# Self attention's rounded rows: turned as float32 with the rounding constant in them, and the maxima scaled by ScalarE

## The chip, the cores and the metric

The kernel runs on one core of one Trainium2 chip. The metric is the device time of one execution in microseconds (us), as the median of several runs. The engines are named as in the profile: PE is TensorE (PEld is its weight load), DVE is VectorE, ACT is ScalarE, POOL is GpSimd, SP is SyncE, which only issues transfers.

## The reference, cut to what matters

The model is a decoder of two layers on 16 sequences of 128 tokens and 512 features: a state space layer, a cross attention and a feed-forward layer, then a self attention, a gated cross attention and a mixture of experts; after each the input is added and a layer norm taken. The change lies in the self attention alone. It has 16 query heads and 4 key and value heads of 32 features, and its four projections are "bitlinear": weights of -1, 0 and 1 times a scale, and activations rounded to 8 bits by row.

```python
def bitlinear(x, W):
    sw = jnp.mean(jnp.abs(W)) + 1e-05
    Wq = jnp.clip(jnp.round(W / sw), -1.0, 1.0) * sw
    sx = 127.0 / jnp.clip(jnp.max(jnp.abs(x), axis=-1, keepdims=True), 1e-05, None)
    xq = jnp.clip(jnp.round(x * sx), -128.0, 127.0) / sx
    return jnp.einsum('bsd,od->bso', xq, Wq)
...
scores = jnp.einsum('bkgsd,bktd->bkgst', qg, k) * scale
scores = jnp.where(causal[None, None, None], jnp.asarray(-jnp.inf, scores.dtype), scores)
p = jax.nn.softmax(scores, axis=-1)
out = jnp.einsum('bkgst,bktd->bkgsd', p, v)
...
return bitlinear(out, Wo)
```

## The kernel before, in words

The 16 sequences stay in SBUF as tiles of 128 tokens by 512 features (k.x), and the layers run as stages one after the other: the state space layer, the cross attention, the feed-forward layer (stage_ffn), the two attentions of the second layer together (stage_attention) and the experts.

stage_attention works on 16 pairs of sequences: eight pairs of the class SelfAttention (L1158), then eight of GatedAttention (L1376). Each pair has eight units (two sequences by four groups of heads), and one loop (L1553) walks over all units. In one turn of the loop, unit t has its exponentials taken (exps, on ACT), the unit before has its probabilities turned on PE and copied out of PSUM (turn), the maxima are taken for units t+1 and t+2 where t+1 is even (top, two units at once, on DVE), and the scores are multiplied for units t+2 and t+3 where t+2 is even (scores, on PE). Beside that, jobs written as generators move on by one step in each turn: project() for a pair that begins 14 units ahead of its own units, values() for each half of a pair that is done, and output() at its end. A yield is the end of a step. Tiles come from rings of buffers: a tag with 2 buffers lets the third tile of that tag in only when the readers of the first are done. The order of the instructions on each engine is fixed at compile time by a planner, which starts from the order in which they are written and fills gaps that it expects; where an instruction must not move, the code says so (keep_in_program_order).

The pieces that the change touches:

- levels (L1188) rounds the rows of two sequences to 8 bits. It is called twice for a pair: by project() on the inputs, and by output() on the attention's result, so 16 times. DVE takes the largest magnitude of each row (L1194), works out the scale (L1195 to L1198), and writes x times the scale plus MAGIC, 12582912.0, into the float32 tile q_t (L1203): in float32 this sum has no fraction left, which is the rounding. ACT adds minus MAGIC and writes bfloat16 (tile q_q, L1207). PE turns the eight blocks of 128 by 128 as bfloat16 into one PSUM tile, ptq (L1212), and ACT copies that tile of 128x1024 to SBUF as q_T (L1215). The projections (L1233, L1256, L1368) use q_T as weights.
- The PSUM tag pp has two buffers of one bank. In stage_attention all of these live in it, one after the other: ptq, pkv (L1230), two pq (L1254), ptk (L1270), two pt (L1260), and two po (L1366). The other six banks hold two score tiles of two banks each (sc0 and sc2), the turned probabilities (pt, in a pool of their own) and the attention's product (ao).
- top (L1300) takes the maximum of two units' scores on DVE (L1303) and multiplies it by nal, the negative scale of the row, on DVE (L1304). exps (L1307) uses the result as the bias of its exponentials (L1313). GatedAttention does the same multiplication on ACT (L1476).
- turn (L1322) copies a unit's turned probabilities out of PSUM. Units whose number is a multiple of DVE_TURNS go to DVE (L1330), the others to ACT (L1328). With DVE_TURNS = 4 that is units 0 and 4 of each pair.
- The levels and the projections of pairs 0 and 1 are put into the last part of stage_ffn (attention(), L986). There the tiles have other homes: q_q lies in the ring xn of that stage.

transpose4 (L565) is a helper that turns four blocks of 128x128 with the float32 identity; its instructions all carry L568.

Of the kernel before, what the change touches and what calls it, by code (L numbers as in the profile page):

```python
# [10 lines left out]
F32 = mybir.dt.float32  # L11
BF16 = mybir.dt.bfloat16
# [3 lines left out]
AF = mybir.ActivationFunctionType  # L16
ALU = mybir.AluOpType
# [3 lines left out]
P = 128  # L21
NB = 16
D = 512
KC = D // P
# [540 lines left out]
def transpose4(k, psum_tile, src):  # L565

    for c in range(4):
        k.nc.tensor.transpose(psum_tile[:, c * P : (c + 1) * P], src[:, c * P : (c + 1) * P], k.ident)  # L568
# [56 lines left out]
def stage_xattn(k):  # L625
# [9 lines left out]
    with ExitStack() as ctx:  # L635
# [224 lines left out]
        for t in range(-12, len(units) + 4):  # L860
            for lag, what in ((3, turn), (2, norm), (1, exps), (0, top), (-1, scores)):
                if not 0 <= t - lag < len(units):
                    continue
                b, g, i = units[t - lag]
                st = state[b]
                if what is scores and (g, i) == (0, 0):
                    st.b, st.sc, st.mx, st.pr, st.sm, st.pTs = b, {}, {}, {}, {}, {}
                what(st, g, i)
                if what is turn and i == 1:
                    running.append(outputs(st, g))  # L870
            if t == len(units) - 6:
                running.append(ffn_weights())
            if t == len(units) - 4:
                running.append(prepare_first())
            b, r = divmod(t + 11, U)
            if r == 0 and b < NB:
                running.append(project(b))
            if (t + 13) % (2 * U) == 0 and t > 0 and (t + 13) // (2 * U) < NB // 2:
                running.append(norm_inputs((t + 13) // (2 * U)))
            b, r = divmod(t + 15, U)  # L880
            if r == 0 and b > 0 and b < NB and b % 4 == 0:
                running.append(angles(b // 4))
            advance()
# [80 lines left out]
def stage_ffn(k):  # L964


    nc, tc = k.nc, k.tc
    LAG = 2
    with ExitStack() as ctx:
        wk = ctx.enter_context(tc.tile_pool(name="s3w", bufs=3))  # L970
# [15 lines left out]
        def attention():  # L986

            bit = k.bit_pool
            homes = [
                dict(q_t=(wk, "q_t", 3), q_q=(wk, "xn", 3), al=(bit, "al", 2), nal=(bit, "nal", 2)) for _ in range(2)  # L990
            ]
            homes[0].update(
                q_T=(wk, "xn", 3), kr1=(wk, "q_q", 3), kr2=(wk, "q_T", 3), qr1=(wk, "xn", 3), qr2=(wk, "q_t", 3),
                sv=(bit, "sv", 1), skT=(bit, "skT", 1), sqT=(bit, "sqT", 2),
            )
            homes[1].update(q_T=(k.early, "q_T", 1))
            k.bit_first = [SelfAttention(k, p, (None, Homes(**h), Homes(pp=(po_, "pp", 2)), None, None, None)) for p, h in enumerate(homes)]
            yield from k.bit_first[0].project()
            k.bit_second = k.bit_first[1].project()
            for _ in range(5):  # L1000
                next(k.bit_second)
                yield

        states = []
        for b0 in range(0, NB, 2):
            st = Ctx() if b0 else k.ffn_first
            st.xs = k.x[b0 : b0 + 2]
            states.append(st)
        late, soon = iter(()), attention()

        def hidden(sn, j):
# [38 lines left out]
        for t in range(len(steps) + LAG):  # L1050
            if t < len(steps):
                n, j = steps[t]
# [5 lines left out]
            if t >= LAG:  # L1058
                m, i = steps[t - LAG]
# [98 lines left out]
class SelfAttention:  # L1158
# [4 lines left out]
    HD = 32  # L1163
    SCALE = 1.0 / math.sqrt(HD)
    LAG = 1
    DVE_TURNS = 4

    def __init__(self, k, p, pools):
        self.k, self.nc, self.xs = k, k.nc, k.x[2 * p : 2 * p + 2]
# [18 lines left out]
    def levels(self, ins, out):  # L1188

        nc, small = self.nc, self.k.small  # L1190
        s = small.tile([P, 2], F32, tag="qs2", name="qs")
        out.step = small.tile([P, 2], F32, tag="qst2", name="qst")
        for i, x in enumerate(ins):
            nc.vector.tensor_reduce(s[:, i : i + 1], x, AX.X, ALU.max, apply_absolute_value=True)  # L1194
        nc.vector.tensor_scalar(s, s, 1e-5, None, ALU.max)  # L1195
        nc.vector.reciprocal(s, s)
        nc.vector.tensor_scalar(s, s, 127.0, None, ALU.mult)
        nc.vector.reciprocal(out.step, s)  # L1198
        yield
        ts = []  # L1200
        for i, x in enumerate(ins):
            ts.append(self.wr.tile([P, D], F32, tag="q_t", name="q_t"))
            nc.vector.tensor_scalar(ts[i], x, s[:, i : i + 1], MAGIC, ALU.mult, ALU.add)  # L1203
        yield
        q = self.wr.tile([P, 2, D], BF16, tag="q_q", name="q_q")
        for i in range(2):
            nc.scalar.activation(q[:, i], ts[i], AF.Identity, bias=self.k.nmagic)  # L1207
        yield
        pt = self.pp.tile([P, 2 * KC, P], BF16, tag="pp", name="ptq")
        for i in range(2):  # L1210
            for c in range(KC):
                nc.tensor.transpose(pt[:, KC * i + c], q[:, i, c * P : (c + 1) * P], self.k.identb)  # L1212
        yield
        out.qT = self.wr.tile([P, 2 * KC, P], BF16, tag="q_T", name="q_T")
        nc.scalar.copy(out.qT, pt)  # L1215

    def project(self):

# [81 lines left out]
    def top(self, n):  # L1300
        nc = self.nc
        mx = self.k.small.tile([P, 2, 4], F32, tag="mx", name="mx")
        nc.vector.tensor_reduce(mx, self.sc2[n], AX.X, ALU.max)  # L1303
        nc.vector.tensor_scalar(mx, mx, self.nal[:, n // 4 : n // 4 + 1], None, ALU.mult)  # L1304
        self.mx[n], self.mx[n + 1] = mx[:, 0], mx[:, 1]

    def exps(self, n):  # L1307
# [14 lines left out]
    def turn(self, n):  # L1322
# [3 lines left out]
        sT = self.sT[n] = self.wk.tile([P, D], F32, tag="at_T", name="at_T", bufs=7)  # L1326
        if n % self.DVE_TURNS:
            nc.scalar.copy(sT, pt)  # L1328
# [47 lines left out]
class GatedAttention:  # L1376
# [7 lines left out]
    LAG = 2  # L1384
    DVE_TURNS = 2

# [210 lines left out]
class Moe:  # L1597
# [95 lines left out]
    def route(self, p):  # L1693
# [27 lines left out]
        for i in range(2):  # L1721
            top = wr.tile([P, 8], F32, tag="r_top", name="r_top", bufs=2)
            nc.vector.max(top, s[:, i])
            nc.vector.match_replace(rest[:, i], top, s[:, i], 0.0)
# [724 lines left out]
```

## Time and profile before

| what | value |
|---|---|
| median of 5 runs | 3019.68 us |
| the five runs | 3001.12, 3001.50, 3019.68, 3021.91, 3023.83 us |
| the profiled execution's own time | 3020.38 us |
| its span | 3018.5 us |
| granted TensorE clock, mean | 0.986 |
| PE busy | 2887.3 us (96%) |
| DVE busy | 1864.2 us (62%) |
| ACT busy | 1335.6 us (44%) |
| POOL busy | 1563.5 us (52%) |

The profile is of one execution, and its time stands 0.7 us above the median. Times inside it are counted from the span's start. The self attention's first scores start at 1659 us and its last exponentials at 1852 us, so nearly all that the change touches lies in 200 us of 3018. The shares of the whole span say little about it; the views by stretch do.

How to read the rows: "x32" is the number of instructions, "mean ns" the duration of one. Instructions of one engine are pipelined, so that one can start before the one ahead of it has ended: what an instruction takes from its engine is the distance from its start to the next one's start, and this is less than its duration. "Idle before" is time in which the engine stood still, with the instruction that ended it.

### The profile page before, as it was taken

How to read it: one execution, taken by the hardware profiler on the slowest of the kernel's cores; microseconds unless marked ns; L12 is line 12 of the kernel's file. 1: busy time of each engine (PE TensorE's matmuls, PEld its weight loads, DVE VectorE, ACT ScalarE, POOL GpSimd, SP SyncE). 2: the span in 40 equal slices, each digit the busy share in tenths (PEclk: the TensorE clock that was granted, in tenths of full speed). 3: DMA queues.
4: the chain of work that ended last, by engine and by line, in shares of the span. 5: the costliest groups of instructions: out<-in, count | busy, mean ns of one | idle time of the engine just before them, and what ended most of it. 6: DMA issues, size and time to landing. Idle time of an engine off the chain costs nothing.

```text
span 3018.5 us, 41723 instructions
## 1 busy us (share of the span) xinstructions
PE 2887.3 (96%) x14446; PEld 1937.2 (64%) x14446; DVE 1864.2 (62%) x4168; ACT 1335.6 (44%) x3297; POOL 1563.5 (52%) x1352
## 2 busy tenths in 40 slices
PE   8999999999999999999999899999999799999988
PEld 6666665555555555555787556666677577777766
DVE  6999997776676686665886897566542312322213
ACT  6887884343343343345444897655422111111112
POOL 7999995434344343332333663266455652343554
PEclk9999999999999999999999999999999999999999
DMA  6755454870000000023000200244366565554653
GB/s 198 216 135 131 134 127 124 282 264 11 7 11 11 7 15 8 11 79 128 1 1 2 69 1 10 66 152 155 132 223 220 204 216 183 188 193 161 206 174 120
DMA packets 177392, 345.23 MB, mean 114 GB/s; under 512 B 25277, under 2 KB 84157, under 8 KB 175638
## 3 DMA queue, kind: packets, MB, share of 16 engines
q1 hardware_dynamic: 126342, 217.64, 23.6%
q0 software_dynamic: 26016, 80.80, 7.9%
q10 hardware_dynamic: 24816, 44.05, 3.9%
q8 instruction: 116, 1.90, 0.3%
q14 instruction: 102, 0.84, 0.1%
HBM read 256.22 MB, written 151.99 MB: 135 GB/s over the span
## 4 chain that ended last, share of the span: by engine, by line
PE 64%; DVE 11%; ACT 3%; issue 2%; another core or an unknown queue 2%; DMA 1%; POOL 1%; SPq 0%; ACTq 0%; DVEq 0%; POOLq 0%
PE y L2069 7%; PE pq L708 7%; PE po L828 6%; PE pu L2033 5%; PE pg L2033 4%; PE po L1040 4%; PE pr L2018 3%; PE ao L817 3%; PE sc L777 3%; PE pt L568 2%; PE pg L1020 2%; PE pu L1020 2%; PE pw L1513 2%; PE ps L1430 2%
## 5 line engine op out<-in xcount | busy, mean ns | idle before, releaser
L797 POOL TENSOR_TENSOR pr<-pr,sm 128x512 f32<-128x512 f32 x128 | 135.3, 1057 | 365.9 <-DVE sm L796 276.9
L66 POOL TENSOR_TENSOR dBx<-dtx,BC 128x1024 f32<-128x1024 f32 (+1 forms) x131 | 300.5, 2315 | 16.6 <-DVE h L66 10.5
L790 ACT ACTIVATE pr<-sc,mx,sf 128x256 f32<-128x256 f32 x256 | 142.2, 560 | 335.5 <-DVE mx L783 296.6
L2092 POOL DMA_INDIRECT got<-results,gidx x126 | 121.0, 961 | 289.0 <-DMA results<-yo 241.6
L66 ACT ACTIVATE h<-dt,negA 128x254 f32<-128x254 f32 x512 | 244.1, 477 | 16.8 <-ACT h L66 0.2
L828 PE MATMUL po<-w,aT 128*128 128x512 f32 x512 | 233.1, 593 | 1.0 <-DVE aT L822 1.0
L708 PE MATMUL pq<-w,xT 128*128 128x512 f32 x512 | 232.0, 596 | 0.0
L2069 PE MATMUL y<-dn,act 128*128 128x512 f32 x372 | 183.2, 616 | 22.6 <-DVE act L2053 13.8
L2104 POOL TENSOR_TENSOR x<-got,x 128x512 f32<-128x512 f32 x134 | 168.4, 1273 | 68.1 <-DMA got<-results,gidx 64.9
L2053 DVE TENSOR_TENSOR act<-pu,act 128x512 f32<-128x512 f32 (+1 forms) x53 | 33.1, 625 | 259.0 <-PE pu L2033 149.7
L679 POOL TENSOR_TENSOR m<-m,m 128x512 f32<-128x512 f32 x96 | 122.5, 1276 | 116.9 <-DVE m L674 113.6
L66 DVE TENSOR_TENSOR_SCAN h<-h,dBx 128x1024 f32<-128x1024 f32 x72 | 164.9, 2290 | 28.0 <-ACT h L66 23.0
L2033 PE MATMUL pu<-xgT,gu 128*128 128x256 f32 (+1 forms) x848 | 174.0, 359 | 0.0
L2033 PE MATMUL pg<-xgT,gu 128*128 128x256 f32 (+1 forms) x848 | 170.4, 354 | 0.0
L66 PE MATMUL pkv<-w,cT 128*128 128x512 f32 x368 | 167.5, 598 | 0.8 <-DMA w<-in_x_wvT 0.5
L1030 POOL TENSOR_TENSOR lo<-sg,hi 128x512 fp32r<-128x512 f32 x64 | 84.2, 1317 | 155.0 <-ACT hi L1029 155.0
L708 PEld LDWEIGHTS pq<-w,xT 128*128 128x128 f32 x512 | 94.7, 191 | 101.5 <-issue 93.8
L2086 DVE TENSOR_SCALAR yo<-y,row 128x512 f32<-128x512 f32 x87 | 65.2, 750 | 152.5 <-PE y L2069 146.3
L828 PEld LDWEIGHTS po<-w,aT 128*128 128x128 f32 x512 | 94.6, 190 | 100.9 <-issue 97.3
L1832 POOL DMA_INDIRECT bucket<-r_row,r_to x126 | 125.2, 994 | 59.4 <-issue 46.9
L2033 PEld LDWEIGHTS pu<-xgT,gu 128*128 128x128 f32 x848 | 145.6, 195 | 15.1
L2033 PEld LDWEIGHTS pg<-xgT,gu 128*128 128x128 f32 x848 | 145.9, 191 | 14.6
(462 smaller groups left out, 6955.8 us busy)
## 6 DMA issues: line engine op xcount, KB each, us to landing
bucket<-zeros SPq DMA_DIRECT2D x88, 388.0 KB
BC<-bcd SPq DMA_DIRECT2D x128, 256.0 KB
row<-bucket SPq DMA_DIRECT2D x39, 776.0 KB
gu<-in_moe_guT SPq DMA_DIRECT2D x16, 1408.0 KB
results<-yo ACTq DMA_DIRECT2D x87, 256.0 KB
x_k<-kv ACTq DMA_DIRECT2D x32, 256.0 KB
x_v<-kv ACTq DMA_DIRECT2D x32, 256.0 KB
v<-x_v SPq DMA_DIRECT2D x32, 256.0 KB
```

The source lines that it names most:

```text
L66: return self.tc.keep_in_program_order(call(*args, **kw))
L679: nc.gpsimd.tensor_tensor(m1, m1, m2, ALU.add)
L708: nc.tensor.matmul(ps, src[:, c], w[c], start=c == 0, stop=c == KC - 1)
L790: nc.scalar.activation(pr[:, j], st.sc[g, i][:, j], AF.Exp, scale=st.sf[:, h : h + 1], bias=st.mx[g, i][:, j : j + 1], accum_out=sm[:, j : ...
L797: nc.gpsimd.tensor_tensor(pr, pr, sm.unsqueeze(2).to_broadcast([P, 2, 2 * P]), ALU.mult)
L828: nc.tensor.matmul(st.po, aT[:, j], k.wo[h // 8][:, h % 8], start=h == 0, stop=h == G * J - 1)
L1020: nc.tensor.matmul(p[:, e], w[:, c, at : at + P], sn.qT[:, :, c], start=c == 0, stop=c == KC - 1)
L1832: return self.nc.gpsimd.indirect_dma_start(out=table[:, :], out_offset=bass.IndirectOffsetOnAxis(ap=to[:, i, g : g + 1], axis=0), in_=row[ ...
L2033: self.nc.tensor.matmul(ps[:, e, 0:n], gu[:, c, at : at + P], u.xT[:, c, 0:n], start=c == 0, stop=c == KC - 1)
L2069: self.k.tc.keep_in_program_order(self.nc.tensor.matmul(y, aT, dn[:, c], start=c == 2, stop=c == 1))
L2092: self.nc.gpsimd.indirect_dma_start(out=got[:, :], out_offset=None, in_=table, in_offset=bass.IndirectOffsetOnAxis(ap=at, axis=0),)
L2104: self.nc.gpsimd.tensor_tensor(self.k.x[b], got, self.k.x[b], ALU.add)
```

## The change

levels no longer makes q_q. PE turns the float32 rows q_t, MAGIC still in them, four blocks to a PSUM tile of 128x512 float32; ACT reads each of the two tiles out of PSUM, adds minus MAGIC and writes the bfloat16 q_T. The number of steps stays: before, a step each for ACT's rounding, for the turning, and then the copy; now a step for the first turning, then the first copy with the second turning, then the second copy. Two pp tiles are taken in place of one. The multiplication of the maxima moves from DVE to ACT. DVE_TURNS goes from 4 to 8, so that only unit 0 of a self attention pair is copied by DVE. GatedAttention has its own DVE_TURNS (2) and its own top, and both stay.

```diff
@@ attention() in stage_ffn
-                dict(q_t=(wk, "q_t", 3), q_q=(wk, "xn", 3), al=(bit, "al", 2), nal=(bit, "nal", 2)) for _ in range(2)
+                dict(q_t=(wk, "q_t", 3), al=(bit, "al", 2), nal=(bit, "nal", 2)) for _ in range(2)
@@ class SelfAttention
-    DVE_TURNS = 4
+    DVE_TURNS = 8
@@ levels
-        q = self.wr.tile([P, 2, D], BF16, tag="q_q", name="q_q")
+        out.qT = self.wr.tile([P, 2 * KC, P], BF16, tag="q_T", name="q_T")
         for i in range(2):
-            nc.scalar.activation(q[:, i], ts[i], AF.Identity, bias=self.k.nmagic)
-        yield
-        pt = self.pp.tile([P, 2 * KC, P], BF16, tag="pp", name="ptq")
-        for i in range(2):
-            for c in range(KC):
-                nc.tensor.transpose(pt[:, KC * i + c], q[:, i, c * P : (c + 1) * P], self.k.identb)
-        yield
-        out.qT = self.wr.tile([P, 2 * KC, P], BF16, tag="q_T", name="q_T")
-        nc.scalar.copy(out.qT, pt)
+            pt = self.pp.tile([P, D], F32, tag="pp", name="ptq")
+            transpose4(self.k, pt, ts[i])
+            yield
+            nc.scalar.activation(
+                out.qT[:, KC * i : KC * i + KC], pt.rearrange("p (c t) -> p c t", c=KC), AF.Identity, bias=self.k.nmagic
+            )
@@ top
-        nc.vector.tensor_scalar(mx, mx, self.nal[:, n // 4 : n // 4 + 1], None, ALU.mult)
+        nc.scalar.mul(mx, mx, self.nal[:, n // 4 : n // 4 + 1])
```

## The prediction

> **What bounds the kernel now.** I read the page's busy shares and chain first.
>
> ```profile
> PE 2887.3 (96%) x14446; PEld 1937.2 (64%) x14446; DVE 1864.2 (62%) x4168; ACT 1335.6 (44%) x3297; POOL 1563.5 (52%) x1352
> ...
> PE 64%; DVE 11%; ACT 3%; issue 2%; another core or an unknown queue 2%; DMA 1%; POOL 1%; SPq 0%; ACTq 0%; DVEq 0%; POOLq 0%
> ```
>
> Over the whole span PE carries the end. The 11% of DVE must lie somewhere, so the next view is busy time by stretch: the end of the feed-forward stage, the middle of the self attention, four pairs' worth of it, and its end.
>
> ```profile
> 1590.00:1660.00 70.00, 68.78 (x464) 54.71 (x463) 45.93 (x111) 28.32 (x48) 26.11 (x22) 1.00 0.01 2
> 1700.00:1817.00 117.00, 105.92 (x892) 68.24 (x893) 113.98 (x311) 111.90 (x273) 82.56 (x116) 1.00 0.01 1
> 1724.00:1817.00 93.00, 84.41 (x708) 54.30 (x705) 92.12 (x261) 89.01 (x218) 63.16 (x90) 1.00 0.01 1
> 1817.00:1852.60 35.60, 34.77 (x236) 22.34 (x229) 26.92 (x97) 26.78 (x67) 12.03 (x20) 1.00 0.01 2
> ```
>
> After the length the columns are PE, PEld, DVE, ACT and POOL. In the first and last row PE is full (1.2 and 0.8 us idle). In the 117 us between, DVE is: 0.9 us idle in 93, where ACT has 4.0 and PE 8.6. The chain of waits over 1700 to 1835 agrees: its shares by line begin with the maxima (L1303) at 15.1%, and seven of the next eight names are DVE's. In order of time it reads like this (start, length, what):
>
> ```profile
> 1763.90 0.66 DVE qr L1182 x2
> 1764.56 1.13 DVE mx L1303
> 1765.69 0.66 DVE x L1370
> ```
>
> So **DVE sets the pace from 1700 to 1817**, one pair in 93/4 = 23.3 us, five pairs' worth; before and after it PE does.
>
> **The change, part by part.** The groups that it touches, by line and shape, in 1724 to 1817 (busy us and mean ns of one behind the bar):
>
> ```profile
> L1207 ACT ACTIVATE q_q<-q_t,nmagic 128x512 bf16<-128x512 f32 x14 | 10.2, 795 | 0.0
> ...
> L1215 ACT COPY q_T<-ptq 128x1024 bf16<-128x1024 bf16 x8 | 8.7, 1090 | 0.0
> ...
> L1304 DVE TENSOR_SCALAR mx<-mx,nal 128x8 f32<-128x8 f32 x16 | 5.5, 341 | 0.0
> ...
> L568 PE MATMUL pt<-ident,qr 128*128 128x128 f32 x32 | 5.0, 279 | 0.0
> ...
> L1212 PE MATMUL ptq<-identb,q_q 128*128 128x128 bf16 x56 | 4.3, 220 | 0.0
> ```
>
> Instructions overlap their neighbours, so I price each by its share of its engine: start to next start in the timeline, averaged over these 93 us. In DVE's timeline:
>
> ```profile
> 1761.83 0.67 DVE L1180 TENSOR_TENSOR qr<-pq,l_cos 128x512 f32<-128x512 f32 x1
> 1762.43 0.21 DVE L1304 TENSOR_SCALAR mx<-mx,nal 128x8 f32<-128x8 f32 x1
> 1762.56 0.74 DVE L1182 TENSOR_TENSOR qr<-pq,l_sin 128x256 f32<-128x256 f32 x2
> ```
>
> The scaling took 0.13 us of DVE here, and another one at 1766.28 took 0.33; their average is 0.257. That of the copy L1330 is 0.598.
>
> *DVE, for four pairs:* 16 scalings leave (16 x 0.257 = 4.1 us) and four of the eight copies (4 x 0.598 = 2.4). Sum -6.5.
>
> *ACT, for four pairs:* eight copies of 128x1024 leave, 0.965 of the engine each: -7.7. The 16 constant-removals stay but read PSUM. None of that shape is here; below stands the plain 128x512 copy out of PSUM (L1344, 0.47), above q_q itself (0.62). The gate's activation L1453, also 128x512 out of PSUM with a pointer operand, took 1882.83 to 1883.40, and I take its 0.57: -0.8. Four copies come from DVE at 0.49: +2.0. The gated attention has the scaling on ACT already (L1476, median 301 ns of 32); in ACT's timeline there:
>
> ```profile
> 1855.95 0.30 ACT L1476 ACTIVATE mx<-mx,r 128x8 f32<-128x8 f32 x1 [2.14 <-DVE mx L1475]
> 1856.34 0.46 ACT L1484 ACTIVATE at_s<-sc,mx,r 128x128 f32<-128x128 f32 x1
> ```
>
> The exponential that reads the result starts 0.39 us after it. Where other work comes between, I bound it below by 0.25 (the 128x128 scalings L1237); I take 0.325, so +5.2 (4.0 to 6.4). Sum -1.3, with ends -4.2 and +0.7. ACT goes from 89.0 to 87.7 of the 93.
>
> *PE, for four pairs:* 64 bfloat16 turnings at 0.067 become float32 ones. The float32 turnings pt took 0.115 and those of the probabilities, some waits in them, 0.144, so +3.1 to +4.9 us; I take 3.1, since pt is the row without probabilities to wait for. PE goes from 84.4 to 87.5.
>
> *Waits.* ACT's scaling must wait for the reduction, as the exponentials do now for L1304 (8.3 us in 11 waits from 1661 to 1853). Behind a scaling that waits stand copies out of PSUM, and PE's turnings and DVE wait for those. In the gated rows ACT stood idle 44.1 us before 21 of 32 scalings, but there it is half empty. Here it ends at 94%, so bounds are 0 and 32 reductions of 1.13 us, 36 us. I take 0: the scaling comes one DVE instruction earlier than now (L1304 stood behind a 0.60 us L1180 above), and this pays for the hop. q_t is now held until PE has turned it, a step longer; its two buffers are refilled three steps later at the earliest, so this costs nothing; if that cover went, the one wait now at L1203 was 0.5 us. The shorter chain from q_t to q_T (one hop less) gains nothing either: project() begins 14 units ahead. The new pp tile is the second rival below. The change issues no transfer and moves past none.
>
> *One rule against it.* The row says that a scaling takes 0.257 of DVE and 0.325 of ACT. The Trainium skill, "ScalarE: Activation LUTs", section "Rules for kernel authors", says to put multiplications on VectorE and not on ScalarE, since VectorE is the faster at them. On the engine's time alone trace and rule agree in sign (+0.07 us each, 1.1 for four pairs). By the rule the edit would be a loss of that much, by the trace it is a gain, because DVE is the engine that is full.
>
> **The sum.** DVE alone would allow 6.5 less in 93 us. But PE at 87.5, with the 2 us in 93 that it idles even where it bounds (1.2 in 70, 0.8 in 36), cannot go below 89.5. So **PE is late next**: 93 - 89.5 = 3.5 us for four pairs, and 3.5 x 117/93 = 4.4 us from 1700 to 1817. Against this, the levels that lie where PE is full already: the inputs of pairs 0 and 1 (1590 to 1660) and about two outputs after 1817. Four levels of eight turnings at 0.048 more: +1.5 us. Net -2.9: 3020.4 - 2.9 = **3017.5** for the profiled execution. That one stood 0.7 above the median; I leave it at 3017.5. The bounds of the price rows move it little: PE's upper end (+4.9) leaves a gain of 2.2 in the middle and a loss of 2.5 at the edges, so no change; DVE's whole 6.5 is a gain of 8.2 - 1.5 = 6.7. Own range 3012 to 3023.
>
> **The rivals.**
>
> *The freed DVE is used whole* (10%). If PE's 87.5 is too high, because its turnings hide behind matmuls of small rows, DVE's 6.5 counts in full, and the part of the stage from 1661 to 1700 gains its share too (DVE 30.6 of 38.6 us occupied there, so little): 3020.4 - 6.7 - 1 = 3012.7. Against it: the busy row above leaves PE 8.6 us, and 5 of them would have to vanish.
>
> *The pp ring takes the place of DVE* (14%, slower). Ten pp tiles a pair become twelve, in two buffers, with PE's queue in order. By the steps of the jobs, two tiles are taken in the same turn in five of eight turns (before, in three), so the first queries (L1256) come to wait for the reader of the tile before. Such waits stand in the list already:
>
> ```profile
> PE pq L1256 <- DVE kr L1244: 2.2, 3, 1.0
> ...
> PE po L1368 <- ACT skT L1275: 1.3, 2, 0.9
> ```
>
> They are 0.65 to 1.0 us each (sum, count, longest). If each of the 32 float32 tiles (16 levels by two) costs 1.0 us of PE, PE in 1661.4 to 1852.6 needs 175.4 + 6.1 (128 x 0.048) + 32 = 213.5 of 191.2 us: +22, so 3042. It decides from 0.3 us a tile, where PE is just full (191.2 - 181.5 = 9.7, over 32), and is slower by more than 0.5% from 0.77. Against it: a tile's reader is written ahead of the next tile's turning.
>
> *Nothing is left* (12%). ACT's upper end, or some of its 36 us of waits, eats DVE's gain: ACT at 89.7 with its present 4.0 idle is again 93.7. Time 3020.4 + 0.7 x 117/93 + 1.5 = 3022.8, up to 3030 if six scalings wait for a whole reduction.
>
> *The other group of runs* (18%). The five runs are two at 3001 and three at 3020 to 3024, and one trace cannot say why. If the median falls among the lower, it is 3001.5 - 2.9 = 2998.6.
>
> **How the numbers follow.** The forecast has 46%. 0.5%, about what a measurement of this kernel can tell from no change, is 15 us. Faster by more than that is only the lower group, 18%; slower only the ring, 14%; the rest, 68%, is within. The range reaches from the lower group with a few us below it (2996) to the end of "nothing is left" (3030), and leaves the ring out.
>
> **What would show it.** Right: between 1700 and 1817 DVE falls from 98% to about 95%, PE rises to 97%, the distance between maxima of neighbouring pairs falls from 23.3 to about 22.4 us; turnings of q_t take 0.115 of PE; ptq to q_T takes about 0.57 on ACT; no 128x1024 copy is left. Wrong: PE's waits for the reader of a pp tile grow by over 10 us (the ring), ACT's idle time before L1304 exceeds the present 8.3 us by as much, or the time moves in the expert stage, which the change does not touch.

## The result, and the profile after

The changed kernel took 3027.39 us (median), the kernel before 3016.46 beside it: a ratio of 1.0035, 95% interval [1.0028, 1.0042]. By the ratio that is 10.6 us slower, against a forecast of 2.9 us faster. The profiled execution took 3030.22 us with a span of 3028.3 (before 3020.38 and 3018.5). Below, times inside a kernel come from its one profiled execution, and ratios from repeated runs beside the kernel before.

The page of the changed kernel, busy times by engine:

```profile
PE 2898.4 (96%) x14446; PEld 1945.2 (64%) x14446; DVE 1852.6 (61%) x4128; ACT 1333.8 (44%) x3321; POOL 1565.5 (52%) x1352
```

DVE has 40 instructions and 11.6 us of work less, as designed, and the kernel is longer all the same. The place is found with the starts of the maxima. The first of the self attention starts at 1661.4 before and 1661.7 after, the last at 1846.2 and 1857.6. What follows agrees again: first to last maxima of the gated attention 282.8 and 282.7 us, from there to the end 881.0 and 880.5. So the whole loss, 11.1 us, lies **between the first and the last maxima of the self attention** (1.1 us of it come back before the first gated maxima). Three of the prediction's stretches, after (PE, PEld, DVE, ACT, POOL, granted clock):

```profile
1700.00:1817.00 117.00, 106.65 (x839) 67.06 (x838) 99.83 (x276) 104.74 (x273) 78.47 (x108) 1.00 0.00 1
1724.00:1817.00 93.00, 85.22 (x671) 53.59 (x670) 81.69 (x234) 83.42 (x218) 60.23 (x85) 1.00 0.00 1
1817.00:1852.60 35.60, 33.28 (x211) 23.48 (x210) 24.31 (x71) 26.02 (x68) 14.73 (x24) 0.90 0.00 1
```

The second row is the one to read. DVE went from 92.12 busy of 93 to 81.69, and **no other engine took its place**: PE 85.22, ACT 83.42. Nothing is full any more, so the time is in waits. (The last row's clock of 0.90, 1.00 before, is taken up below.) The largest waits from 1700 to 1825, before and then after (sum, count, longest):

```profile
POOL at_h L1316 <- ACT at_s L1313: 32.6, 24, 2.8
...
ACT at_s L1313 <- DVE mx L1304: 3.1, 7, 0.6
```

```profile
POOL at_h L1313 <- ACT at_s L1310: 30.9, 19, 4.8
DVE sm L1347 <- POOL at_p L1314: 15.1, 8, 3.4
PEld pts L568 <- ACT at_T L1325: 8.9, 15, 1.1
...
ACT mx L1301 <- DVE mx L1300: 8.0, 9, 1.6
```

Lines behind L1204 stand three lower in the changed kernel. New on DVE in this stretch is a wait of its row sums (sm) for POOL's products of the probabilities. On ACT the wait for the maxima now stands before the moved scaling, 8.0 us in place of 3.1. The chain of waits of the changed kernel goes round from engine to engine (start, length, what):

```profile
1725.95 1.09 DVE mx L1300
1727.83 0.80 ACT at_s L1310 x2
1729.11 0.72 ACT at_s L1310 x2
1729.90 1.02 POOL at_h L1313
1731.50 1.68 POOL x_wg L1153
1735.89 1.75 DVE qs L1194 x3
1739.15 1.13 DVE mx L1300
```

Where DVE followed DVE before, maxima now wait for exponentials, these for the next engine, and POOL's share of the probabilities stands in a queue behind an unrelated product (x_wg, 1.68 us).

The price tags are not what failed. The changed groups, after, from 1724 to 1817 (busy, mean ns):

```profile
L1210 ACT ACTIVATE q_T<-ptq,nmagic 128x512 bf16<-128x512 f32 x16 | 11.3, 708 | 0.0
...
L568 PE MATMUL ptq<-ident,q_t 128*128 128x128 f32 x64 | 9.9, 277 | 0.0
...
L1301 ACT ACTIVATE mx<-mx,nal 128x8 f32<-128x8 f32 x15 | 4.7, 312 | 6.9 <-DVE mx L1300 6.9
```

Counted from start to next start, as in the prediction, one of each took 0.573, 0.124 and 0.228 us of its engine.

**The order changed too.** The planner fixes the order at compile time, and it chose anew. These are DVE's lists between successive maxima of the self attention, one letter for an instruction (S row sums, o outputs scaled, x outputs added, n norm statistics, L norm, q row magnitudes, c copy of turned probabilities, r rope; others left out), behind the 11th to the 18th maxima:

```
before  xxnonqS  cLL     oSq     crr  xonxqnS  cqq  LLoSqc  rr
after   xSxonnq  LL      Soqqqc  rr   xSxnonq  LL   Soqqqc  rr
```

In the groups that begin with x, the row sums S ended the list before, when POOL was done; after, S stands second, with five instructions and the next maxima queued behind it.

### The profile page after: what moved, and what is told of

Same layout as the page of the kernel before. It is cut to its first block, busy times and chain, and to the rows that moved or that the text cites. A ratio compares the mean times of both kernels' runs of the same rounds, so it can differ in the third digit from the quotient of the medians.

```text
span 3028.3 us, 41711 instructions
## 1 busy us (share of the span) xinstructions
PE 2898.4 (96%) x14446; PEld 1945.2 (64%) x14446; DVE 1852.6 (61%) x4128; ACT 1333.8 (44%) x3321; POOL 1565.5 (52%) x1352
## 3 DMA queue, kind: packets, MB, share of 16 engines
q1 hardware_dynamic: 126342, 217.64, 23.6%
## 4 chain that ended last, share of the span: by engine, by line
PE 75%; DVE 12%; ACT 4%; DMA 2%; issue 2%; POOL 2%; another core or an unknown queue 2%; SPq 0%; ACTq 0%; DVEq 0%; POOLq 0%
PE y L2066 7%; PE pq L708 7%; PE po L828 6%; PE pkv L66 5%; PE pu L2030 5%; PE pg L2030 4%; PE po L1040 4%; PE pr L2015 3%; PE ao L817 3%; PE sc L777 3%; PE py L66 3%; PE pt L568 2%; PE ps L1427 2%; PE pd L66 2%; PE pg L1020 2%
## 5 line engine op out<-in xcount | busy, mean ns | idle before, releaser
L66 POOL TENSOR_TENSOR dBx<-dtx,BC 128x1024 f32<-128x1024 f32 (+1 forms) x131 | 300.6, 2317 | 16.8 <-DVE h L66 10.2
L1829 POOL DMA_INDIRECT bucket<-r_row,r_to x126 | 124.8, 991 | 59.2 <-issue 47.1
```

The costliest lines, as they stand in the source:

```text
L66: return self.tc.keep_in_program_order(call(*args, **kw))
L1829: return self.nc.gpsimd.indirect_dma_start(out=table[:, :], out_offset=bass.IndirectOffsetOnAxis(ap=to[:, i, g : g + 1], axis=0), in_=row[ ...
```

## The experiments

Seventeen more kernels ran, in five groups. The kernels of a group share a chip and its runs of before (medians 3015.9, 2962.5, 3014.6, 3023.4 and 3021.2 us), so only ratios are compared across groups. Beside the ratio stands the **stretch**, from the 9th to the 29th maxima of the self attention, five pairs' worth, and the **tail**, from the 29th to the 32nd. The stretch repeats well: 125.0 and 125.1 us in two executions of the changed kernel, 116.0 twice for after_in_before_order, on two chips. Stretch and tail are of one execution each, and the ratio covers the whole kernel, so the columns need not agree to the microsecond.

| kernel | ratio [95%] | stretch, us | tail, us |
|---|---|---|---|
| before (profile of the start) | 1 | 118.2 | 23.6 |
| after (profile of the result) | 1.0035 [1.0028, 1.0042] | 125.0 | 28.2 |
| only_levels | 1.0046 [1.0028, 1.0063] | 124.0 | 24.1 |
| only_turns | 1.0001 [0.9987, 1.0015] | 120.1 | 24.3 |
| only_top | 1.0033 [1.0019, 1.0046] | 130.5 | 24.4 |
| after_pinS | 1.0025 [1.0011, 1.0039] | 127.2 | 23.8 |
| top_in_before_order | 0.9998 [0.9989, 1.0007] | 119.6 | 23.8 |
| before_in_top_order | 1.0030 [1.0019, 1.0041] | 128.4 | 26.3 |
| levels_in_before_order | 1.0013 [1.0005, 1.0022] | 118.9 | 24.0 |
| after_in_before_order | 1.0015 [1.0006, 1.0024] | 116.0 | 25.4 |
| before_own_order | 1.0002 [0.9990, 1.0014] | 118.4 | 23.6 |
| after_again | 1.0029 [1.0018, 1.0040] | 125.1 | 28.2 |
| after_in_before_order_2 | 1.0007 [0.9993, 1.0020] | 116.0 | 25.4 |
| no_top_in_before_order | 1.0030 [1.0019, 1.0041] | 119.0 | 29.7 |
| after_dve_order | 1.0022 [1.0007, 1.0037] | 122.2 | 24.9 |
| after_pe_order | 1.0061 [1.0041, 1.0080] | 127.7 | 25.2 |
| after_act_order | 1.0052 [1.0032, 1.0072] | 126.8 | 28.0 |
| after_pool_order | 1.0052 [1.0032, 1.0072] | 127.6 | 25.0 |
| no_turns_in_before_order | 1.0016 [0.9998, 1.0033] | 116.5 | 24.5 |

**First group: one part at a time, and one wait pinned.** Three theories went in: A, the planner's new order puts DVE's row sums too early, where they wait for POOL; B, the second ring tile of each level holds PE up; C, the moved scaling's wait on ACT holds up what is queued behind it. The edits, each to one kernel:

```diff
# only_levels: before, with the change's levels and its home without q_q (as in the diff above)
# only_turns: before, with
-    DVE_TURNS = 4
+    DVE_TURNS = 8
# only_top: before, with
-        nc.vector.tensor_scalar(mx, mx, self.nal[:, n // 4 : n // 4 + 1], None, ALU.mult)
+        nc.scalar.mul(mx, mx, self.nal[:, n // 4 : n // 4 + 1])
# after_pinS: after, with
-        nc.vector.tensor_reduce(sm.rearrange("p j g -> p g j"), self.part[i], AX.X, ALU.add)
+        self.k.tc.keep_in_program_order(nc.vector.tensor_reduce(sm.rearrange("p j g -> p g j"), self.part[i], AX.X, ALU.add))
```

> The kernel before with the new levels alone (float32 turnings, constant off in the copy); maxima on DVE, DVE_TURNS 4. Before is 3016.5 us, after 3027.4. Theory A (order: the planner has moved the row sums L1350, which wait for POOL, ahead of other DVE work that stands before the next maxima): here the planner still puts the row sums last before the maxima in most pairs, so 3014 to 3019, and DVE's wait for at_p stays near the 10 us of before. Theory B (the pp ring and the dearer turnings on PE): the whole loss is here, 3025 to 3029. Theory C (the scaling on ACT waits, and holds up the copies behind it): nothing here, 3014 to 3018.

> The kernel before with DVE_TURNS 8 alone: one copy of 0.6 us per pair moves from DVE to ACT. A: the order of row sums and maxima is nearly that of before, so 3013 to 3018. B: 3016, no ring is touched. C: ACT gets 0.5 us more per pair and the maxima stay, 3016 to 3018.

> The kernel before with the maxima's scaling on ACT alone. A: the planner puts the row sums ahead of four or five other DVE instructions in six of eight pairs, as in the changed kernel, so it has most of the loss, 3022 to 3027, with DVE waiting over 18 us for at_p. B: no loss, 3014 to 3018. C: the whole loss, 3025 to 3029, with ACT idle before its scaling as in the changed kernel (17.9 us), and DVE's wait for at_p a result of it.

> The changed kernel, and the row sums (the reduction of part in values) kept in the written order on DVE, so that they cannot be moved ahead; all three parts of the change stay. A: DVE no longer waits for at_p (under 6 us in place of 24) and the time falls to that of before or below it, 3008 to 3018. B: 3025 to 3029, the ring is as it was. C: 3025 to 3029, the scaling is still on ACT.

Two parts that share no instruction, levels and top, each cost the whole loss alone (1.0046 and 1.0033), and together they cost no more (1.0035). Prices that belong to instructions would add up. (Of only_levels the trace shows 6.1 us more in the self attention and 3.7 in the gated one, so not all of its ratio is explained by the place found above.) Pinning the row sums in their written place took their wait from 29.2 us to nothing, yet the stretch stayed at 127.2: DVE then waited elsewhere (18.6 us idle). So theory A in its narrow form, the row sums alone, fell. B, the ring of PSUM tiles, cannot explain only_top, which takes no tile more, and C, waits on the moved scaling, cannot explain only_levels, which moves none. Two theories were left: the **order** of all the lists, or the **parts** by some cost of their own.

**Second group: the instructions of one kernel in the order of another.** In these kernels one function more runs behind stage_attention's code; it ties each instruction to the next of its engine's list without adding a wait on the chip. ORDER holds the other kernel's lists from 1585 to 1880 us; where a kernel has the new levels, the planner still places the new turnings and their copies. The traces show DVE, ACT and POOL in the order asked for, all through the stretch.

```diff
         stage(k)
+        if stage is stage_attention:
+            in_order(k)
...
+def in_order(k):
...
+    for engine, order in ORDER.items():
+        row = [rows[engine][i] for i in order]
+        for one, then in zip(row, row[1:]):
+            k.tc.add_manual_dep(then, one.name, info, reason="order")
```

> The instructions of only_top (scalings on ScalarE, eight VectorE turnings, levels as in before), but from the end of the feed-forward stage to the end of the self attention every engine is held to the order of before (added scheduling edges between neighbours; the moved scaling stands on ACT where its place on DVE was, the moved copies by their start in before). Order theory: only_top lost 10 us because the planner gave all engines another, looser order; in the order of before its time is that of before or a few us less: 3008 to 3018, eight maxima-to-maxima steps from the 9th to the 29th in 114 to 119 us. Parts theory: the scaling on ACT and the four copies on ACT cost waits by themselves: 3025 to 3030, stretch 126 to 131 us.

> The instructions of before unchanged, each engine held through the same stretch to the order that the planner gave only_top (the scaling back on DVE behind its maxima, the copies back on DVE). Order theory: slow like only_top or worse, since DVE has its old load again: 3024 to 3035, stretch 125 to 135 us. Parts theory: the order matters little, 3012 to 3019, stretch 117 to 121 us.

> The instructions of only_levels (float32 rows turned, the constant taken off in two copies out of PSUM; scalings and turnings as in before), held to the order of before except the new turnings ptq and the two copies that read them, which the planner still places. Order theory: 3013 to 3020 (PE has 3 us more work in four pairs, DVE the same). Parts theory: the second ptq tile in the two pp buffers and the longer turnings cost by themselves, 3025 to 3030.

> All instructions of after, held to the order of before through the stretch, the new ptq turnings and their copies placed by the planner. Order theory: what I had forecast for the change, some 3 us below before, 3008 to 3016, stretch 112 to 118 us (before 118.2, after 125.0), and faster than after by about 10 us. Parts theory: like after or above, 3025 to 3031.

What the first two expectations say of turnings and copies was an error of mine: only_top moves the scalings and nothing else.

The first pair is the clean one. The same instructions cost 1.0033 in the planner's order and 0.9998 in the order of before; the instructions of before, untouched, cost 1.0030 in the order of only_top. The 9th and the 29th maxima of before, and of before_in_top_order (start, duration):

```profile
1704.39 1.22 DVE L1303 TENSOR_REDUCE mx<-sc 128x8 f32<-128x1024 f32 x1 [0.30 <-PE sc L1297]
...
1822.61 1.21 DVE L1303 TENSOR_REDUCE mx<-sc 128x8 f32<-128x1024 f32 x1
```

```profile
1704.92 1.23 DVE L1303 TENSOR_REDUCE mx<-sc 128x8 f32<-128x1024 f32 x1 [0.56 <-PE sc L1297]
...
1833.27 1.21 DVE L1303 TENSOR_REDUCE mx<-sc 128x8 f32<-128x1024 f32 x1
```

118.2 us have become 128.4 with not one instruction changed. And the waits of before_in_top_order from 1700 to 1825 carry the mark of the changed kernel, the row sums behind POOL:

```profile
POOL at_h L1316 <- ACT at_s L1313: 40.0, 23, 5.3
DVE sm L1350 <- POOL at_p L1317: 11.5, 6, 4.3
```

Part of the 128.4 is PE's clock: from 1758.1 to 1761.5 and from 1829.8 on it was granted by half, by an estimate 3.5 us of PE's work inside the stretch. The changed kernel's stretch above had the full clock throughout (1.00), so its 6.8 us more than before are not the clock's.

So the **order theory stands** for the scaling, in both directions. For the full change it stands in the middle: the stretch is 116.0 us instead of 125.0, even shorter than before's. Its two maxima:

```profile
1702.93 1.23 DVE L1300 TENSOR_REDUCE mx<-sc 128x8 f32<-128x1024 f32 x1 [1.68 <-PE sc L1294]
...
1818.91 1.21 DVE L1300 TENSOR_REDUCE mx<-sc 128x8 f32<-128x1024 f32 x1
```

But the time did not follow all the way: 1.0015 where 3 us below before was expected. The expectation failed by that much, and levels_in_before_order (1.0013) says the same of the levels alone: the order carries most of the loss, and a small rest stays. Whether that rest is the parts' own cost, or due to the places that the planner gave to the new turnings, these runs do not tell.

**Third group: a control, and the rest.**

```diff
# before_own_order: before, held to its own lists
# after_again: the changed kernel as it is
# after_in_before_order_2: the same kernel as after_in_before_order
# no_top_in_before_order: after without the moved scaling, held to the order of before
-        nc.scalar.mul(mx, mx, self.nal[:, n // 4 : n // 4 + 1])
+        nc.vector.tensor_scalar(mx, mx, self.nal[:, n // 4 : n // 4 + 1], None, ALU.mult)
```

> The instructions of before, held through the stretch to before's own order by the same kind of scheduling edges: the control of the method. Nothing is to change: ratio 0.999 to 1.001, stretch from the 9th to the 29th maxima about 118 us. Its profile stands beside the others of the same chip.

> The changed kernel as it is, on the chip of this call. Order theory and parts theory both: ratio 1.002 to 1.005 to the kernel before; stretch about 125 us. It gives the pair to the next run.

> The changed kernel held to the order of before once more. The first time it was 1.0015 and its stretch 116.0 us, so the stretch gained and the whole lost. If that loss of 4 us is the parts' (48 ns more TensorE work for each of 128 turnings is 6.1 us, and TensorE is the bound from the end of the feed-forward stage on and in the gated attention), the self attention ends 2 to 4 us before that of before_own_order, and the gated attention gives this back: its last maxima at the same time or later. If it is the chip's scatter, the ratio is 0.998 to 1.001 here.

> The change without the moved scaling (levels and eight VectorE turnings... that is DVE_TURNS = 8, four copies of turned probabilities less on VectorE), held to the order of before with the new turnings free. ACT has 8.5 us less and 2.0 more in four pairs, DVE 2.4 less, PE 3.1 more. If an unloaded ACT is worth something in that order: 0.998 to 1.000; if PE's added 6.1 us count as in the full change: 1.001 to 1.002.

Holding an order costs nothing by itself (1.0002, stretch 118.4). The changed kernel in the order of before is 1.0007 [0.9993, 1.0020] this time, so whether a rest of 2 to 4 us is left is at the edge of what can be told. Its two traces say what happens to the gain: from the first to the last self maxima it took 185.5 and 185.7 us, before 184.8, since the 2.2 us won in the stretch are lost ahead of it (44.1 and 44.3 against 43.0 from the first to the 9th maxima) and in the tail (25.4 against 23.6). Behind that, from the first to the last gated maxima, the kernels with the new levels took longer than those of the same chip without them, all held to the order of before: 281.3 and 282.0 us against 278.1 (top_in_before_order), and 283.0 and 285.1 against 280.6 (before_own_order). These are single traces, and phases of half clock differ among them. no_top_in_before_order missed its expectation: its stretch is 119.0 but its tail 29.7, and 10.2 us at half clock from 1824.9 go with that (more on this behind the fifth group).

**Fourth group: which engine's list.** After, with one engine alone held to the order of before, the planner free with the rest (here for DVE, the lists of the others taken out of ORDER):

```diff
 ORDER = {
...
-    "PE": [
...
-    "Activation": [
...
-    "Pool": [
```

> The changed kernel, VectorE alone held to the order of before through the stretch; the planner orders the rest around it. After is 1.003 with 125 us from the 9th to the 29th maxima; with all four engines held 1.0007 to 1.0015 and 116.0. If VectorE's list is what was lost (it had 91 of 118 us of the chain in before): 116 to 119 us and 1.000 to 1.002. If it is another engine's: 122 to 128.

> The changed kernel, TensorE alone held to the order of before (the new turnings free). If TensorE's list is what was lost: 116 to 119 us; if another's, 122 to 128.

> The changed kernel, ScalarE alone held to the order of before (the new copies free; scalings where they stood on VectorE). If ScalarE's list is what was lost, the place of the scalings and of the exponentials above all: 116 to 119 us; if another's, 122 to 128.

> The changed kernel, GpSimd alone held to the order of before. The chain of after between the 9th and 29th maxima has 44 us of GpSimd (bf16 halves of the probabilities behind rope and weight products), where before had VectorE. If GpSimd's list is what was lost: 116 to 119 us; if the 44 us only follow from the other engines' order: 122 to 128, hardly changed.

None of the four reaches 116 to 119. DVE's list alone brings back 2.8 of the 9.0 us (125.0 to 122.2), the others nothing or less. As far as runs can tell in which the planner ordered the rest anew, the loss is **in the fit of the lists to each other**; no one list carries it.

**Fifth group: the copies.** after_in_before_order with

```diff
-    DVE_TURNS = 8
+    DVE_TURNS = 4
```

> The change without the moved copies (DVE_TURNS stays 4): float32 levels and scalings on ScalarE, held to the order of before with the new turnings and their copies free. VectorE is 4.1 us lighter in four pairs, ScalarE about 3.3 lighter (8.5 less, 5.2 more), TensorE 3.1 heavier. If the full change in that order gave nothing because the four copies load ScalarE at the end of the self attention (from the 29th to the last maxima 25.4 us against 23.6), this one is faster than both kernels: 0.997 to 0.999. If the levels' work on TensorE is what eats the gain, 1.000 to 1.002. If a pause of TensorE lets its clock fall again in the last pairs, as in after (half clock from 1832 to 1839), 1.002 or more, and the clock column shows it.

The ratio, 1.0016 [0.9998, 1.0033], has before inside its interval. Leaving the copies out gained nothing that shows, so nothing here points to them as what ate the gain. No kernel here is shown to be faster than before.

**A second cost, seen in the traces: PE's clock.** The tails in the table fall in two groups, 23.6 to 26.3 and 28.0 to 29.7. The changed kernel around 1830 (the columns of the stretches; PE first, the clock third from the end):

```profile
1829.00:1831.00 2.00, 0.38 (x1) 0.00 (x0) 1.97 (x5) 1.98 (x7) 1.50 (x3) 1.00 0.00 0
1831.00:1832.00 1.00, 0.67 (x6) 0.67 (x7) 1.00 (x4) 1.00 (x4) 0.00 (x0) 1.00 0.00 0
1832.00:1839.00 7.00, 7.00 (x35) 5.82 (x34) 4.18 (x10) 6.09 (x18) 2.51 (x5) 0.53 0.00 1
```

PE stands nearly still for 2 us, and then its granted clock is 0.53 on average for 7 us, in which it is full. By an estimate from the last row, 7 x 0.47 = 3.3 us of PE's work is lost, where PE is the bound; the tail grew by 4.6 us. What made it stand still is in PE's timeline (idle time and its releaser in brackets):

```profile
1829.66 0.38 PE L1290 MATMUL sc<-mask,identb 128*128 128x512 bf16 x1 [0.68 <-ACT at_s L1310]
1831.34 0.66 PE L568 MATMUL pt<-ident,x 128*128 128x128 f32 x4 [1.29 <-DVE xT L1410]
```

A turning waited 1.29 us for DVE's copy xT, which DVE began at 1830.60, behind the maxima of 1829.46. The three kernels with long tails (after twice, after_act_order, no_top_in_before_order) show a pause there and a clock of 0.74 to 0.83 over 1820 to 1840; among those with short tails only only_top (0.91) and before_in_top_order (0.83, tail 26.3) show a drop there, and half of it or more lies ahead of their tails, which begin at 1832.0 and 1833.3. The pause alone does not make the drop. after_dve_order has the same one, and the clock stays whole:

```profile
1826.00:1828.00 2.00, 0.38 (x1) 0.00 (x0) 2.00 (x4) 2.00 (x7) 1.18 (x2) 1.00 0.00 0
1828.00:1835.00 7.00, 6.97 (x53) 5.83 (x57) 5.38 (x15) 6.84 (x20) 2.67 (x5) 1.00 0.02 4
```

So has after_pool_order (0.38 of 2.0 us from 1830 to 1832). Their tails are 24.9 and 25.0 us, those of the changed kernel 28.2: by an estimate from these, about 1 us of the 4.6 goes with the pause and 3 us with the half clock. This is a reading of traces: no run held the clock up to test it.

## Why the prediction was wrong

- **What bounds the kernel** was read rightly as far as it goes: DVE was full from 1700 to 1817. What it meant was not. As the held runs read, DVE was full because the lists of all engines fitted so closely that it hardly waited; it was not merely the engine with the most work. When the scalings left DVE in the very same order (top_in_before_order), its idle time in the stretch rose from 2.7 to 7.3 us and the stretch from 118.2 to 119.6 (3.4 us of it at half clock, from 1733.0). Freed time turned into waits.
- **The unit prices held.** Occupied time in the stretch, scaled from five pairs to four: DVE (125.0 - 17.4) - (118.2 - 2.7) = -7.9, so -6.3 (forecast -6.5). ACT (125.0 - 13.4) - (118.2 - 5.9) = -0.7, so -0.6 (forecast -1.3, with ends -4.2 and +0.7). A scaling took 0.228 us of ACT, below my lower end of 0.25; q_T 0.573 (0.57); a float32 turning 0.124 (0.115). PE came out higher, (125.0 - 10.8) - (118.2 - 10.9) = +6.9, so +5.5, over my upper end of +4.9; but with the same instructions in the order of before it was occupied for 107.3 and 108.3 us against the 107.3 of before, under my lower end of +3.1, so this sum tells how closely its matmuls follow each other as much as what they cost. (One reading was off and changes nothing: from 1661.4 to 1700 DVE was busy for 31.5 of 38.6 us, not 30.6.)
- **The failed step is "Waits. [...] I take 0".** I bounded them by 0 and 36 us and chose 0, since the scaling "comes one DVE instruction earlier than now" and "this pays for the hop". That argues with the order of before, and the order of before was gone. After has 14.7 us more idle DVE in the stretch (17.4 against 2.7), about twice what its lighter load had freed; the wait for the maxima on ACT went from 8.3 to 17.9 us in the whole self attention, 9.6 more, just short of the 10 that my own sign of an error named ("exceeds the present 8.3 us by as much"), and DVE's row sums waited 29.2 us for POOL (10.3 before), a wait that the prediction does not name. I had written in my own description that a planner fixes the order, and priced no new order. Of what was to show the forecast right, DVE busy at about 95% and PE at 97% from 1700 to 1817, the first row above has 99.83 and 106.65 of 117, 85% and 91%; the distance from pair to pair became 25.0 us (125.0/5), not 22.4.
- **"PE is late next", worth 4.4 us,** was not seen. In the planner's order PE idled 10.8 of 125.0 us. In the order of before it idled 8.6 and 7.6 of 116.0, and the stretch gained 2.2, where the forecast of 3.5 in 93 makes 4.4 in 118.2. No engine was full there (DVE idle 6.9 and 7.3, ACT 5.5), so what sets that pace is left open.
- **The edges, +1.5:** in the order of before, the first eight maxima and the tail cost 1.1 and 1.8 us more than before, 2.9 together, some of which may be copies and waits and not the turnings alone. Held to the order of before, the kernels with the new levels came out at 1.0007 to 1.0030, those without at 0.9998 and 1.0002. That fits PE's added work, and it is not separated further.
- **The rivals.** The freed DVE was not used whole. The pp ring was not it: only_top loses as much with no tile more. "Nothing is left" came nearest in the time (up to 3030), by the wrong road: it saw some scalings wait, and only_levels, without a moved scaling, loses as much. The group of low runs was no property of the kernel; runs of before spread over 3000.5 to 3027.5.
- **The rule weighed against it**, from the Trainium skill, "ScalarE: Activation LUTs", section "Rules for kernel authors" (multiplications on VectorE rather than ScalarE), is not decided by these runs: the scaling on ScalarE cost nothing to speak of in a kept order (0.9998) and 1.0033 in a new one.

## What to carry to other kernels

Where a planner or scheduler orders the instructions, an edit is two changes: the work, and a new order. Before pricing the first, compare the new lists with the old; if they differ, run the edited instructions in the old order and the old instructions in the new one, and only then say what the edit costs. An engine at 99% in a stretch may show a close fit between lists; taking work off it gains nothing unless the others can be ready earlier as well.

## What the runs showed of the hardware

- Behind a pause of TensorE of about 2 us its granted clock was half for 7 us in the changed kernel, and whole behind the same pause in after_dve_order (the rows above), so the length of the pause does not settle it. In the clock records of all these traces, from 1580 to 2200 us, a phase of half clock lasted 3.4, 6.8, 10.2 or, once, 17.1 us. In before one stood in the self attention (0.56 over 1668 to 1675), at the start of the pairs. In before_own_order, with the same lists, it lasted longer after a pause at the same place, and from the first to the 9th maxima it took 47.1 us instead of 43.0:

```profile
1668.00:1669.00 1.00, 0.04 (x1) 0.00 (x0) 1.00 (x2) 1.00 (x5) 0.92 (x2) 0.53 1.04 393
1669.00:1684.00 15.00, 14.89 (x72) 10.01 (x71) 11.19 (x23) 10.55 (x26) 7.68 (x12) 0.50 0.50 155
```

- The Trainium skill, "TensorE: Matmul & The Clock Gate", section "Part 1: The HAM clock gate (the "warmup" mystery)", gives about 3.4 us of idling before the clock is halved and about 3.4 us of work before it is whole again. The rows here show it halved behind 2 us in which PE worked 0.38, and half for 7 and for about 16 us with PE full; here the measurement decides.
- On one of the chips the kernel before took 2962.5 us, on the others 3014.6 to 3023.4. The self attention's stretch does not differ (116.0 us for after_in_before_order on that chip and on another); from the last gated maxima to the end, in the experts' stage, the same kernel took 830.6 and 869.6 us.
